# Three rewritten passages and 109 unread TensorE products in a twelve-block residual kernel on one core

## The chip, the core and the metric

The kernel runs on one core of one Trainium2 chip. The metric is the device time of one execution in microseconds (us), lower is better. The kernel before was run three times: 3741.72, 3752.7 and 3753.8 us; the median is 3752.7 us.

The engines are named as the profile names them: PE is TensorE (matrix products and transposes; PEld is its loading of weights, that is, of the operand that stays in place), DVE is VectorE, ACT is ScalarE, POOL is GpSimd, and SP is SyncE, whose queue issues most of the transfers (DMAs) between memory and the core's SBUF. Products land in PSUM, from where DVE or ACT copy ("evict") them into SBUF.

## The reference

The input `x` is [16, 64, 256], that is 1024 tokens of 256 features; there is a context `ctx_1024` of [16, 1601, 256] and a mask over it. The reference adds twelve blocks to `x`, each of a layer norm of `x`:

```python
x = x + _L0_xattn_ref(_layernorm(x), ctx, ctx, ...)    # 16 heads, softmax over the 1601 context rows
x = x + _L0_attn_ref(_layernorm(x), ...)               # 4 encoder layers, linear attention with elu + 1
x = x + _L0_ffn_ref(_layernorm(x), ...)                # 8 experts, the best 2 of each token, capacity 160
x = x + _L1_xattn_ref(_layernorm(x), ctx, ...)         # slot attention, 3 rounds with a GRU cell
x = x + _L1_attn_ref(_layernorm(x), ...)               # 16 heads, softmax over 64 tokens, own input added
x = x + _L1_ffn_ref(_layernorm(x), ...)                # 8 experts, 2 rounds of an integrator, then a refining MLP
x = x + _L2_xattn_ref(_layernorm(x), ctx, mask, ...)   # relu(score + bias)^2, normed by its sum, masked
x = x + _L2_attn_ref(_layernorm(x), ...)               # linear attention over 64 features of normed q and k
x = x + _L2_ffn_ref(_layernorm(x), ...)                # 16 experts, the best 8, and a shared one
x = x + _L3_xattn_ref(_layernorm(x), ctx, ...)         # one head of 256 over the context
x = x + _L3_attn_ref(_layernorm(x), ...)               # 16 heads, causal, with a bias by relative position
x = x + _L3_ffn_ref(_layernorm(x), ...)                # int8 quantised product
```

Three pieces matter for the change. `_L0_attn_ref` begins with `x = sqrt(256) * x_in + position_row` and a second layer norm of that (`ln1` of its first layer), so between block one and the first product of block two stand two layer norms in a row. `_L1_ffn_ref` adds to its experts' products the bias of the chosen expert (`expert_b2`, 8 x 768) or of the shared one (`shared_b2`, 768), and ends with `out = xf + integration_weight * refined`, where `refined = gelu(...) @ refine_w2 + refine_b2`. `_L3_attn_ref` adds `rel_emb[buckets]` (one number for each pair of positions and each head) to the scores and hides the keys above the diagonal.

## The kernel before, in words

The 1024 tokens are 8 tiles of 128 (`NT`), the 256 features 2 chunks of 128 (`KC`). `x` stays in SBUF for the whole program as `self.x` [128, 8, 256]. The program is one method for each block, in the order of `STAGES`; the last block (`l3_ffn`) runs inside `l3_attn`. Products and transposes are issued by `mm` (L2470) and `tr` (L2476). While `self.pinned` is true they, and the DVE, ACT and POOL instructions issued through the helper `Written` (L50 to L60), keep the order in which they are written; so a profile line of L2472, L2477 or L59 is that of a helper, and the operation is told by the names of its tiles. Each engine works through its own queue in order: an instruction that waits holds back all behind it on that engine. A tile of a pool is one of a fixed number of buffers (`bufs`) with the same tag; making the next one waits until the old one has been read.

**The two blocks that stream the context, l0_xattn (0 to 862 us) and l2_xattn (2338 to 2997 us).** Both go through `stream` (L2361). The 16 batches times 13 chunks of 128 context rows are taken in pairs, k from -9 to 103. Each round writes, in this order: `weights(k+1)` (scores of the next pair, and their exponentials or squares on ACT and DVE), in the last eight rounds one `out(t)` (the output product of token tile t, added to `x` by DVE's `add_to_x`), two `project` (keys and values of a context chunk 18 chunks ahead, evicted from the PSUM tag `bk`), `values(2k)` and `values(2k+1)` (products of the exponentials with the values, into the tag `acc`), and, in l0_xattn only, jobs `extra` (maxima for a coming batch). After the loop come the heads of the last batch and `out(7)`. Before the loop, l0_xattn norms all tiles, transposes them and makes the queries `qT`.

**l0_attn (862 to 1375 us).** The tokens are two halves, a (tiles 0 to 3) and b (tiles 4 to 7); of each half a `Half` holds `x`, `y`, `n` (the normed tiles), `hT` (the transposed ones), `kz`, `va`, `qT`, `h1T`. Steps of both halves are generators that the text lets run by turns (`go(it, n)`): `project` (L560: transposes, keys and values of each tile `kv(t)`, queries), `attend` (L605: `sums` of keys times values, `apply`, output product), `feed` (the MLP), and at the end `route` (L751: the choice of experts, in blocks g = 0 to 3 of two tiles each: a transpose `turn`, a product `gate`, ranks on DVE, a product `pos` for the places, then a scatter by POOL). The start of the block (L825 to L836) measures, scales (`start`, L704) and norms tiles 0 to 3 of a and 0, 1 of b before the first `turn`; the rest of b follows between products of `project(a)`. The weights of layer 0 and the row vectors (`rows`, `lnf`) are transferred on SP's queue as their buffers come free. A tile `zero` [128, 256] is written to all rows of `taken` (the experts' rows in memory) by one transfer.

At the end of l0_attn stands the bias by relative position for block eleven: 16 x 4 small products of one-hot rows `hot` with `rel_emb` into four PSUM banks, then 32 DVE additions of `above` (-3e38 above the diagonal) that evict them, and a transfer to memory by POOL's queue.

**l1_xattn (1400 to 1925 us)** turns the slots (`turned`), then goes through the context of all batches and ends each round with `update` (the GRU). **l1_attn (1925 to 2010 us) and l3_attn (3620 to 3740 us)** share `token_attention` (L2498): `linear(0)` norms and transposes half 0 (`tr`), makes queries and keys (`lin_t`) and values; then, for each tile t, `scores(t)`, parts of `linear(1)`, `values(t-1)` (transposes `turn` of the weights, then the products `acc`), and `project(t-2)`. In l1_attn `own_input` is true. In l3_attn a `then` object interleaves the last block: `Then.turn` (L2287, transposes `trb` of the quantised tile) and `Then.product`. **l2_attn (2997 to 3106 us)** has the same form: `linear` (L1881), `key_features`, `apply`, `sums`, `project` (L1992).

**l1_ffn (2010 to 2338 us)** loads its weights on SP's queue in the order of the code. After them it makes `bias2` [128, 768] in bf16 (L1551 to L1563): rows 0 to 23 hold the 8 experts' biases split into three bf16 parts, rows 24 to 26 the shared one. A float32 tile `raw` of 32 rows gets the biases three times, and DVE takes nine steps over 32 x 768: a copy into bf16, the rest, and a masked addition, three times. `pc`, the first product that reads it, is in `control`. `refine` (L1730) ends the block: for each tile four products `po`, DVE's addition of `fb2` (`refine_b2`), POOL's product with `iw` (`integration_weight`), DVE's addition to `x`, and the measuring of `x` for the next layer norm.

## Time and profile before

| | before |
|---|---|
| median of the runs | 3752.7 us |
| lowest and highest run | 3741.72 and 3753.8 us |
| the profiled execution | 3741.89 us |
| its span in the profile | 3740.1 us |
| mean granted clock of TensorE in it | 0.963 |
| PE busy | 3434.1 us (92%) |
| DVE busy | 1975.9 us (53%) |
| ACT busy | 1459.0 us (39%) |
| POOL busy | 1284.7 us (34%) |
| transfers | 259.71 MB, mean 69 GB/s |

A profile is that of one execution. Its slice row PEclk gives, for 40 equal stretches of the span (93.5 us each), the clock that was granted to TensorE in tenths of full speed, and the row PE its busy share; the same can be asked for any stretch. The row of a single stretch gives its bounds and length, the busy time (number of instructions) of PE, PEld, DVE, ACT, POOL and SP, then the granted clock, the busy share of the DMA engines and GB/s. A row of the timeline gives the start, the duration, the engine, the line, the operation with its tiles (output, then inputs, then partitions x elements) and the number of instructions in the group, and in brackets the idle time of the engine before it with what ended it.

### The profile page before, as it was taken

To read this page: it belongs to the slowest core of one execution; us is meant where nothing else is said; L and a number is where in the kernel's file an instruction comes from. 1 tells how busy PE (TensorE), PEld (TensorE's weight loads), DVE (VectorE), ACT (ScalarE), POOL (GpSimd) and SP (SyncE) were. 2 spreads that over 40 slices of the span, in tenths; PEclk is the share of its full clock that TensorE was granted. 3 is DMA by queue.
4 is the path that set the end of the run, shared out by engine and by line. 5 is a ranking of instruction groups with operands and counts; after the bars stand their busy time and mean duration, and the time that the engine had idled before them with its cause. 6 is when DMAs were issued, how large, how long until landed. Compare 5 with 4: busy or idle time off the path is not lost.

```text
span 3740.1 us, 70775 instructions
## 1 busy us (share of the span) xinstructions
PE 3434.1 (92%) x30951; PEld 2183.0 (58%) x30966; DVE 1975.9 (53%) x3682; ACT 1459.0 (39%) x2081; POOL 1284.7 (34%) x786
## 2 busy tenths in 40 slices
PE   8999999996999977999987998999999879999986
...
PEclk9999999998999978999998999999999979999997
...
DMA packets 106411, 259.71 MB, mean 69 GB/s; under 512 B 9235, under 2 KB 74515, under 8 KB 103798
## 3 DMA queue, kind: packets, MB, share of 16 engines
...
q14 instruction: 66, 0.54, 0.0%
...
## 4 chain that ended last, share of the span: by engine, by line
PE 49%; DVE 8%; ACT 3%; issue 2%; POOL 0%; DMA 0%; another core or an unknown queue 0%; SPq 0%; DVEq 0%; POOLq 0%; ACTq 0%
PE pk L2472 9%; PE sc L2472 8%; PE pu L2472 4%; PE acc L2472 3%; PE gate L2065 3%; PE up L2065 3%; PE lin L216 3%; PE pc L1688 3%; PE prz L2472 2%; PE gelu_t L1605 2%; PE turn L2477 2%; PE lin L2472 1%; PE pa L2472 1%; PE pn L2472 1%; DVE e L1832 1%
## 5 line engine op out<-in xcount | busy, mean ns | idle before, releaser
L2405 POOL TENSOR_TENSOR tot<-tot,e 128x1024 f32<-128x1024 f32 (+1 forms) x340 | 802.9, 2362 | 374.7 <-ACT e L349 251.5
L292 DVE TENSOR_REDUCE m<-sc 128x4 f32<-128x2048 f32 x96 | 220.1, 2293 | 272.6 <-PE sc L2472 271.5
L1832 DVE SCALAR_TENSOR_TENSOR e<-sc,row_L_xattn_nbias,free 128x2048 f32<-128x2048 f32 x104 | 244.3, 2349 | 116.5 <-PE sc L2472 114.9
L1834 ACT ACTIVATE e<-e 128x2048 f32<-128x2048 f32 x104 | 198.7, 1911 | 243.7 <-DVE e L1832 243.7
L349 ACT ACTIVATE e<-sc 128x2048 f32<-128x2048 f32 x104 | 195.2, 1877 | 242.3 <-PE sc L2472 240.7
L2472 PE MATMUL sc<-qb,kT 32*128 32x128 f32 x6656 | 245.4, 284 | 35.3 <-DVE m L306 12.4
L2472 PEld LDWEIGHTS sc<-qb,kT 32*128 32x128 f32 x6656 | 206.4, 187 | 79.7 <-issue 24.1
L2472 PE MATMUL acc<-e,v 128*32 128x128 f32 x6656 | 226.9, 276 | 7.2 <-ACT e L1835 7.2
L2472 PEld LDWEIGHTS acc<-e,v 128*32 128x32 f32 x6656 | 170.3, 110 | 106.6 <-issue 95.2
L2472 PE MATMUL pk<-cT,wk 128*128 128x512 f32 (+1 forms) x512 | 206.6, 532 | 3.6 <-DVE rows L322 3.6
L2472 PE MATMUL pk<-wv,cT 128*128 128x256 f32 x832 | 209.6, 394 | 0.0
L1835 ACT ACTIVATE e<-e 128x2048 f32<-128x2048 f32 x104 | 198.8, 1911 | 3.2
L2472 PE MATMUL pk<-wkv,cT 128*128 128x256 f32 x832 | 196.3, 386 | 0.0
L2472 PE MATMUL pk<-cT,wkv 128*128 128x512 f32 (+1 forms) x512 | 194.9, 522 | 0.0
L2472 PEld LDWEIGHTS pk<-wv,cT 128*128 128x128 f32 x832 | 149.5, 190 | 76.4 <-issue 59.0
L2472 PEld LDWEIGHTS pk<-wkv,cT 128*128 128x128 f32 x832 | 153.2, 190 | 28.5 <-issue 4.3
L2472 PE MATMUL pu<-cn,e 128*64 128x257 f32 (+1 forms) x1248 | 145.0, 389 | 12.9 <-POOL e L1240 12.9
L1688 PE MATMUL pc<-ew,eh 128*128 128x256 f32 x640 | 155.5, 385 | 0.0
L2069 ACT ACTIVATE g<-gate 128x512 f32<-128x512 f32 x68 | 40.7, 598 | 293.3 <-PE gate L2065 293.3
L2472 PE MATMUL sc<-kT,qb 32*128 32x512 f32 (+2 forms) x1536 | 141.5, 468 | 14.6 <-DVE m L292 2.3
L1230 POOL TENSOR_TENSOR e<-e,mx 128x512 f32<-128x512 f32 x96 | 81.8, 883 | 195.1 <-DVE mx L1229 195.1
L2472 PE MATMUL sc<-cT,qT 128*64 128x512 f32 (+1 forms) x768 | 142.4, 523 | 3.5 <-ACT scs L1210 3.0
...
## 6 DMA issues: line engine op xcount, KB each, us to landing
cT<-in_ctx_t SPq DMA_DIRECT2D x128, 832.0 KB
...
```

What stands on the lines that cost most here:

```text
L216: nc.tensor.matmul(pm, xT[:, k, t * P : (t + 1) * P], w[:, k, :], start=(k == 0), stop=(k == kc - 1))
L292: nc.vector.tensor_reduce(x.m4[:, g, :, i], pm, AX.X, ALU.max)
L349: nc.scalar.activation(e, pm, AF.Exp, scale=0.25)
L1230: pin(nc.gpsimd.tensor_tensor(p.e, p.e, p.mx.unsqueeze(2).to_broadcast(p.shape), ALU.subtract))
L1605: nc.tensor.matmul(pm, w[:, c, lo : lo + m], cT[:, c, :], start=(c == 0), stop=(c == nk - 1))
L1688: nc.tensor.matmul(pc[:, n, j, :], s.eh[i][:, c, tok], ew2[:, c, cols], start=False, stop=(c == 3))
L1832: nc.vector.scalar_tensor_tensor(e16, pm16, nb, free[:, at : at + P].unsqueeze(1).to_broadcast([P, 16, P]), ALU.add, ALU.mult)
L1834: nc.scalar.activation(e, e, AF.Relu)
L1835: nc.scalar.activation(e, e, AF.Square)
L2065: nc.tensor.matmul(pm[-1], w[:, k, n * P : (n + 1) * P], xT[:, k, tok], start=(k == 0), stop=(k == KC - 1))
L2405: nc.gpsimd.tensor_tensor(tot[:w], x.first if c == 1 else tot[:w], e[:w], ALU.add)
L2472: ins = self.nc.tensor.matmul(*args, **kw)
```

## The change

The change has two kinds of edits; what the program computes stays the same.

**Unread products.** A new function `awake(pool, n, tag)` takes one PSUM buffer of the pool and multiplies the identity with the first 512 columns of the constants into it, n times; nothing reads the buffer. These products are written in at 37 points of the run, each ahead of the work that PE would come to next, 109 products in all: 5 (with a tile of ones in place of the identity) ahead of the first transposes of the program, 2 before the first scores of l0_xattn, 3 (l0_xattn) and 7 (l2_xattn) in the last rounds of the stream and 3 more before each one's last `out`; in l0_attn 10 in the first layer's `project_first`, `project` and `attend` and 14 in `route`; 21 in l1_xattn; in l1_attn 4 before the transposes and 3 in `values`, in l3_attn 3 before `lin_t` and 5 in `values`; 12 in l2_attn; and 14 in `Then.turn` before tiles 0, 6 and 7.

**Three rewritten passages.**

1. The seam from l0_xattn to l0_attn. The buffers `y` and `hT` of half a and the small ones of the norms are made before l0_xattn (`begin`). `out(t)` now measures its tile; after tile 5 the roots for tiles 0 to 3 are worked out on DVE (`quick_roots`, without ACT's root) and tiles 0 and 1 are scaled and measured (`start`), after tile 6 they are normed (`norm`), after tile 7 transposed and evicted into `hT` (`turned`). In l0_attn half a begins with `project_first` in place of `project`: `kv` of tiles 0 and 1 at once, then the transposes of tiles 2 and 3, `kv` of these, then one exponential over all four tiles and the queries. The norms of tiles 2, 3 and 4 to 7 are written between its steps. The tiles are made, and the row vectors transferred, in another order; `zero` becomes [128, 128] with two transfers of half rows, and POOL's two additions of `lnf` to `x` are moved behind the first `mix`.

2. The bias by relative position. Four products of the identity with `above` start the four banks, the 64 small products add to them, and 16 ACT copies evict in place of 32 DVE additions.

3. l1_ffn. The biases are loaded first, once, in 128 rows of 54 columns, split by DVE in five steps of that size, and brought into the rows of `bias2` by two pairs of transfers through memory on POOL's queue. `fb2` is multiplied by `iw` and added to `x` by POOL in `start`, so that `refine` multiplies by `iw` as it evicts, and POOL's product is gone.

The diff, cut to its core:

```diff
+    def awake(self, pool, n, tag, bufs=None):
+        if n:
+            pm = pool.tile([P, 512], F32, tag=tag, name="awake", **({"bufs": bufs} if bufs else {}))
+            for _ in range(n):
+                self.mm(pm, self.ident, self.cst[:, :512], start=True, stop=True)

 l0_xattn
+        self.begun = self.begin(self.at_once.enter_context(tc.tile_pool(name="l0y", bufs=1, reuse_waits="tile")))
...
+            nc.vector.memset(qT[:, 0, :512], 1.0)
+            pm = ps.tile([P, 512], F32, tag="acc", name="awake")
+            for _ in range(5):
+                self.mm(pm, qT[:, 0, :P], qT[:, 0, :512], start=True, stop=True)
             self.layernorm(sb, self.x, xln)
...
             def weights(pair):
                 pm = quad()
+                if pair[0][0].b == pair[0][1] == 0:
+                    self.awake(ps, 2, "acc")
...
+            def start():
+                n = sb2.tile([P, KC, SKP], F32, tag="cT", name="n")[:, 0, : 2 * D].rearrange("p (t d) -> p t d", d=D)
+                for t in range(2):
+                    nc.scalar.activation(n[:, t], self.x[:, t, :], AF.Identity, bias=nx.less[:, t : t + 1])
+                    nc.vector.scalar_tensor_tensor(nx.y[:, t, :], n[:, t], nx.r[:, t : t + 1], pos, ALU.mult, ALU.add)
+                    nx.measure(nx.y[:, t, :], nx.mvy[:, t])
+            def norm():
+                nx.root(nx.ry, nx.mvy, 1.0)
+                for t in range(2):
+                    nc.vector.tensor_scalar(
+                        nx.n[:, t], nx.y[:, t, :], nx.mvy[:, t, 0:1], nx.ry[:, t : t + 1], ALU.subtract, ALU.mult)
+            def turned():
+                pt = ps.tile([P, KC, 2, P], F32, tag="bk", name="tr")
+                ... four transposes
+                nc.vector.tensor_scalar(to[:, 0], of[0], ln_s[:, 0:1], ln_b[:, 0:1], ALU.mult, ALU.add)
+                nc.scalar.activation(to[:, 1], of[1], AF.Identity, bias=ln_b[:, 1:2], scale=ln_s[:, 1:2])
...
             def out(t):
                 self.add_to_x(t, pm)
+                self.measured(t, False)
+                if t == 5:
+                    nx.quick_roots(0, 4)
+                    start()
+                if t == 6:
+                    norm()
+                if t == 7:
+                    turned()

 l0_attn
+            def project_first(s, w):
+                for t in range(HT):
+                    if t == 2:
+                        self.awake(ps, 1, "mm", 3)
+                        turn(s, 1, w.ln1_s, w.ln1_b)
+                        yield
+                    self.awake(ps, (1, 0, 4, 0)[t], "mm", 3)
+                    kv(t)
+                    yield
+                A.activation(s.tmp, s.kz, AF.Exp, bias=less)
+                for c in range(KC):
+                    pm = by_feature(w.wq, c, s.hT)
+                    ...
+                    yield
+                add_row(s, w.bo)
...
-            for s, n in ((a, 2), (b, 1)):
-                for p in range(n):
-                    start(s, p)
-                    measure(s, s.y, p)
-                for p in range(n):
-                    norm(s, s.y, p)
...
-            pr = project(a, w)
-            go(pr, 3)
-            measure(b, b.x, 1)
+            pr = project_first(a, w)
+            start(a, 1)
+            nx.roots(4, NT, V, A)
             go(pr, 1)
+            norm(a, a.y, 1)
+            go(pr, 1)
+            start(b, 0)
+            go(pr, 1)
+            norm(b, b.y, 0)
             start(b, 1)
...
-            at, pr = attend(a, w), project(b, w)
+            at, pr = attend(a, w, True), project(b, w, True)    # True: 2 unread products in each
...
 route
+                self.awake(ps, (3, 0, 0, 7)[g], "mm", 3)
                 turn(s, p)
...
+                self.awake(ps, (0, 3, 0, 1)[g], "mm", 3)
                 pos = ps.tile([P, 2, E], F32, tag="mm", name="pos", bufs=3, padded_shape=[P, 64, E])
 position bias
+            for r in range(4):
+                self.mm(banks[r] ..., self.ident, above[:, keys].unsqueeze(2).to_broadcast([P, 16, H]), start=True, stop=False, ...)
...
-                            V.tensor_tensor(
-                                bias[o, :, 2 * g + j, keys], of[:, g], above[o, :, keys].to_broadcast([S, 4, 16]), ALU.add)
+                        A.copy(to[:, j], of)

 l1_xattn
+            self.awake(ps, 9, "tr", 3)
             tiles[0].sT = take(turned(tiles[0].s), "sT", 2)
...
+                self.awake(ps, 0 if n else 7, "tr", 3)
                 update(sa, None, sb_ if n else None)
...
+                    self.awake(ps, 5, "tr", 3)
                 update(sb_, an and an[0])

 l1_ffn
+            raw = sb.tile([P, n8 + W // P], F32, tag="raw", name="raw")
+            ... two loads; for j in range(3): copy into part[:, j], subtract
+                nc.gpsimd.dma_start(split.rearrange("j (p c) -> p j c", p=P), part[:, :, lo : lo + n])
+                nc.gpsimd.dma_start(bias2[at : at + 3 * m], split.rearrange("j (e n) -> (j e) n", n=W))
...
 start (l1_ffn)
+                if s.i == 0:
+                    nc.gpsimd.tensor_tensor(fb2, fb2, iw, ALU.mult)
+                nc.gpsimd.tensor_tensor(s.x, s.x, fb2.unsqueeze(1).to_broadcast([P, TT, D]), ALU.add)
 refine
-                    nc.vector.tensor_tensor(y, pm, fb2, ALU.add)
-                    nc.gpsimd.tensor_tensor(y, y, iw, ALU.mult)
+                    nc.vector.tensor_tensor(y, pm, iw, ALU.mult)

 l2_attn
+                    self.awake(ps, 4 if i == 0 and t0 else 0, "mm", 2)    # before the transposes of z
+                    self.awake(ps, 2 * g, "mm", 2)                        # before pqp
+                    self.awake(ps, 0 if t else 2, "mm", 2)                # before key_features(0)
+                    self.awake(ps, 2 if t > NT else 0, "mm", 2)           # before the last project

 l3_ffn, Then.turn
+                self.awake(ps, {0: 7, 6: 4, 7: 3}.get(t, 0), "mm", 2)

 stream
+        waits = {-1: 3} if extra else {-7: 2, -5: 1, -4: 1, -1: 3}
                 if h and k >= 0:
+                    self.awake(ps, waits.get(k - N // 2, 0), "bk")
                     values(2 * k)
...
         finish(xs[B - 1])
+        self.awake(ps, 3, "bk")
         out(NT - 1)

 token_attention
+            if i == 0:
+                self.awake(ps, 4 if own_input else 0, "mm", 2)            # before the transposes
+                if n == i == 0:
+                    self.awake(ps, 0 if own_input else 3, "mm", 2)        # before lin_t
+            self.awake(ps, ({1: 2, 2: 1} if own_input else {2: 1}).get(t, 0), "mm", 2)     # values, before turn
+            self.awake(ps, 0 if own_input else {1: 1, 2: 1, 5: 2}.get(t, 0), "mm", 2)      # values, before acc
```

## The prediction

> **What bounds the kernel now.** I read the page's busy table and slices first, then the chain that ended last, then the stretches of 1 and 2 us around each dip of the clock, then the timeline of TensorE (PE) there.
>
> ```profile
> span 3740.1 us, 70775 instructions
> PE 3434.1 (92%) x30951; PEld 2183.0 (58%) x30966; DVE 1975.9 (53%) x3682; ACT 1459.0 (39%) x2081; POOL 1284.7 (34%) x786
> ...
> PE   8999999996999977999987998999999879999986
> ...
> PEclk9999999998999978999998999999999979999997
> ...
> PE 49%; DVE 8%; ACT 3%; issue 2%; POOL 0%; DMA 0%; another core or an unknown queue 0%; SPq 0%; DVEq 0%; POOLq 0%; ACTq 0%
> ```
>
> PE is busy 92% and leads the chain; two things eat the rest: about 306 us in which PE is idle, and the low slices of the clock row, at the seams between stages. In 1 us stretches, PE's busy time times the missing share of the clock sums to 99 us over 34 dips: an upper bound for what a clock that never falls could give. One dip in full:
>
> ```profile
> 60.00:62.00 2.00, 2.00 (x11) 0.61 (x10) 0.86 (x5) 0.33 (x1) 0.00 (x0) 1.00 0.05 20
> 62.00:64.00 2.00, 0.75 (x3) 0.10 (x1) 1.77 (x4) 1.25 (x2) 0.00 (x0) 1.00 0.00 0
> 64.00:66.00 2.00, 0.44 (x13) 0.47 (x17) 1.41 (x1) 0.61 (x1) 0.00 (x0) 1.00 0.00 0
> 66.00:68.00 2.00, 2.00 (x36) 1.68 (x28) 0.00 (x0) 0.00 (x0) 0.00 (x0) 0.54 0.03 8
> 68.00:70.00 2.00, 2.00 (x8) 0.80 (x7) 0.00 (x0) 1.25 (x1) 0.00 (x0) 0.61 0.00 0
> 70.00:72.00 2.00, 2.00 (x11) 0.50 (x9) 0.00 (x0) 1.21 (x2) 1.30 (x1) 1.00 0.00 0
> ```
>
> First number after the stretch's length is PE, third from last the clock. PE waits from 62.75 to 65.56, and then works at about half clock for 3.4 us: 1.7 us lost after the wait is over. These waits recur:
>
> ```profile
> 65.56 1.60 PE L2472 MATMUL sc<-qb,kT 32*128 32x128 f32 x32 [2.81 <-DVE m L292]
> ...
> 870.12 0.48 PE L2477 MATMUL tr<-cst,n 128*128 128x128 f32 x1 [5.71 <-DVE n L59]
> ...
> 880.21 6.24 PE L2472 MATMUL lin<-wkv,hT 128*128 128x512 f32 x8 [7.35 <-DVE hT L59]
> ...
> 2039.50 0.40 PE L1681 MATMUL pc<-bias,shared 128*128 128x256 bf16 x1 [7.27 <-DVE bias L1563]
> ...
> 3629.01 3.70 PE L2472 MATMUL lin_t<-xT,wqkv 128*128 128x512 f32 x8 [0.80 <-ACT qb L2549]
> ...
> 3725.25 0.88 PE L2477 MATMUL trb<-identb,f_xq 128*128 128x128 bf16 x4 [4.18 <-ACT f_xq L2283]
> ...
> 3730.07 0.39 PE L2477 MATMUL trb<-identb,f_xq 128*128 128x128 bf16 x2 [0.26 <-ACT f_xq L2283]
> ```
>
> **The price of one unread product.** A float32 product with 512 columns is two records. In the row at 3629 their weights follow each other every 0.43 us at full clock, in the row at 880 every 0.85 at half: 0.86 or 1.71 us a product. I count 109 of them. 78 stand where this trace has a wait of PE, of 86 us together: 67 us at full clock, 78% of the waits. In a wait they cost nothing, since the releaser (a DVE, ACT or POOL chain) doesn't depend on PE; where there is no wait they cost 0.86 each.
>
> **Joined part 1, the seam from l0_xattn to l0_attn.** Before: last product of the stream ends 864.40, first key product 880.21, layer 0's first `sums` 911.06. That head start is the layer norms (DVE and ACT, 863 to 880) of six token tiles, done in a block. After: tiles 0 and 1 are normed during the last three `out` calls, so the first key product waits for four transposes (0.6) and two evictions (0.54 and 0.56) after the last `add_to_x`: about 866.5, 14 us sooner. From there to `sums` PE has 8 key, 2 query and 16 transposing products, 16 us warm; the waits for the norms of tiles 2, 3 and of the second half, interleaved, I put at 8 us, against 13 before. So `sums` comes near 891 to 893: 19. Against it: five more DVE and ACT steps stand in the tail of the stream (ACT's last `exp` ends 857.29, the values need it at 857.9: no slack), and three products stand before those values, 2.6 at most. Value 17, ends 8 (the row of b vectors again lands at 868.7, as now, and four products run after it) and 25. The zeros written in two half rows on SP's queue at 12.8 are read only after 1303; POOL's two additions of 2.5 us moved behind `mix` are read at the last layer.
>
> **Joined part 2, the position bias.** 32 DVE additions (4.55 us) become 16 ACT copies (nearest row: 128x256 copied in 0.37; 16 of half that size about 4) and four identity products (256 columns, 2 records of 0.23 each: 1.8). PE's 128 little products before them take 9.4 at half clock. With seven unread products in the 7.18 us wait before 1345.73, the gate, position and bias products run warm: 1.2 + 2.0 on the chain to the scatter, some 4 before the eviction. The next wait (1367 to 1374, for DVE's copy of xsT) has behind it a softmax that stood until 1369.7 for something the trace does not name; if it is the transfer of the bias, it comes sooner too. Value 4, ends -2 and 8.
>
> **Joined part 3, l1_ffn.** The 7.27 us wait at 2039.50 is DVE's splitting of a 32x768 bias (nine steps of 0.55 to 1.0). In a 128-partition layout the steps are 54 columns wide (nearest rows: 0.15 to 0.2), and two trips through memory follow on POOL's queue; even issued as late as 2006.6, where the raw bias is loaded now, four hops of some 2.5 us end before 2032. Then routing's chain (softmax, ranks: about 5 us on DVE) is next, partly beside four `pc` products: 7, ends 3 and 9. In `refine` the POOL product (0.64 plus two hand-overs) leaves a serial chain of 2.2 us per tile; 1.45 remains, under PE's 1.77: the last tile ends 2 sooner, ends 1 and 2.5. POOL's new addition of 2.35 twice lies before `vn`, which is not read until 2045.
>
> **Unread products in real waits.** Loss of the dip each prevents, discounted a little: stream's start at 66 1.7; routes 1291 5 (of 6.3) and 1318 1.5; l1_xattn 1438 1.5 and 1911 2.2; l1_attn 1929 2.8 and 1966 1.5; end of l2_xattn 2991 2.5; l2_attn 3015 2, 3025 2.6, 3069 3.8, 3107 1; l3_attn 3671 3, 3690 1.5, 3703 2.5. Sum 35. At the start of the program and at 1412.78 (nine products in 8.75) I take 0.5 each: after 1412 ACT stands until 1423.4 on an unnamed queue with the DMA engines full. 36, ends 15 and 50.
>
> **Unread products where I find no wait.** End of l2_xattn: two and one where PE waits 0.57 and 0: 1.5. Between the two transposes and `acc` of value tile 5 of l3_attn: the filler needs the PSUM buffer that ACT empties only at 3703.0, so two start when `acc` could: 1.5. `attend` of layer 0: two, 1.7. The program's end: four before the transposes of tile 6 (row at 3730.07: 0.26 of wait; the 4.18 is before tile 4) and three before tile 7, which must then wait for tile 6's product: about 4. Sum 9, ends 2 and 16.
>
> **Sum.** 17 + 4 + 7 + 2 + 36 - 9 = 57. From this 3 for waits not filled (2.98 at 2101, 2.39 at 2306) that may now fall into a bad phase of the clock: 54. The profiled execution took 3741.89 (span 3740.1 and 1.8 around it): 3688. It is at the lower end of the runs shown (3741.72 to 3753.8, median 3752.7); a median of runs spread like that can lie up to 11 higher, which the upper end takes in.
>
> By the Trainium skill, "TensorE: Matmul & The Clock Gate", section "HAM oscillation — how this bites in real kernels", only idle gaps over about 3.4 us are to be avoided. Then the fillings of 2 to 3 us would give nothing, some 17 less: 3705. The row at 65.56 speaks against it: 2.81 us of wait, and the clock at 0.54 behind it.
>
> **Rivals.** (a) PE stays warm, but the chains of DVE and ACT end the stages anyway (l2_attn, l3_attn: ACT `e`, DVE `rec` 1.76 in each step), so half of the 36 goes back into waits: gain 54 - 18 = 36, and with a seam at its low end 27, about 3712. For: 88 us of waits behind ACT and DVE remain on the chain. Against: after most of these dips PE runs without a wait. (b) Everything fills: 25 + 8 + 11 + 45 - 5 = 84, 3658. (c) Slower: identity products do not hold the clock. Then the 78 take 133 us at half clock in 86 us of waits, 47 over, and the other 31 up to 53 instead of 9; minus the 30 of the joined parts, about 3770 with some of it hidden. It decides from 1.1 us per product on, where 78 fill 86. Against it: PE enters each wait at full clock, which falls only 1 to 4 us later, and transposes by the same identity run amid clock 1.00 (1453 to 1900). (d) No change: seam at 8, filled waits at 15, losses at 16, about 12.
>
> **Chances.** Forecast (gain 40 to 72) 0.58; (a) 0.23; (b) 0.09; (c) 0.07; (d) 0.03. Faster by over 0.3% (11 us, about what can be told) 0.90, same 0.03, slower 0.07. The range leaves out the far half of (b), (c), (d) and little of (a): 3658 to 3728.
>
> **What would show it.** Mean clock from 0.963 to about 0.98. No dip after 66, 1291, 1929, 3015, 3069; dips left at 1374, 2014, 2247, 2339, 3472. First key product within 4 us of the stream's last product; no wait for DVE `bias` in l1_ffn. The rows of the unread products: 0.43 a record. Wrong if they read 0.85, if waits before the same instructions are as long behind the fillers, or if the seam waits on a row transfer.

## The result, and the profile after

The changed kernel's median is 3730.05 us over eight runs (3726.93 to 3733.56); the kernel before, on the same chips, has 3742.65 (3740.18 to 3754.37). The ratio is 0.9969, with a 95% interval from 0.9957 to 0.9981: 12 us faster, where 54 were forecast. The time lies 2 us above the upper end of the range. The profiled execution took 3730.16 us; its span is 11.7 us shorter than that of the kernel before. Executions of one kernel can lie in two groups some 10 to 13 us apart (of ten of `joined_only`, told below, three took 3727 to 3731, one 3735 and six 3741 to 3743), so that a median also says which group was met more often, and I read stretches from the profiled executions.

Of the page of the kernel after, the busy row, the slice row of the clock and the shares of the chain that ended last:

```profile
span 3728.4 us, 71203 instructions
...
PE 3499.4 (94%) x31177; PEld 2200.2 (59%) x31192; DVE 1970.9 (53%) x3645; ACT 1461.2 (39%) x2093; POOL 1286.4 (35%) x784
...
PEclk9999999999999979999999999999999989999998
...
PE 75%; DVE 13%; ACT 7%; issue 2%; DMA 1%; POOL 0%; SPq 0%; ACTq 0%; DVEq 0%; POOLq 0%
```

The clock did what was forecast: its mean is 0.979, and of the low slices three are left, at 7 around 1305 to 1398 us and at 8 around 2983 to 3076 and at the end. PE's busy time went *up* by 65 us, although the only products added that anything reads are the four of the position bias. The dip that the prediction showed in full, in the same view, is gone:

```profile
62.00:64.00 2.00, 1.57 (x4) 0.38 (x2) 2.00 (x2) 1.65 (x2) 0.00 (x0) 1.00 0.00 0
64.00:66.00 2.00, 1.40 (x37) 1.31 (x38) 0.45 (x1) 0.00 (x0) 0.00 (x0) 1.00 0.04 8
66.00:68.00 2.00, 2.00 (x15) 0.95 (x12) 0.00 (x0) 1.28 (x1) 0.00 (x0) 1.00 0.00 0
```

To see where the time went I summed three things over the span in stretches of 1 us: PE's busy time, its idle time, and busy time times the missing share of the clock (the loss by the clock). `joined_only` is the kernel after without its unread products; `squares_first` and `joined_squares` are the same pair with one more edit.

| | span | PE busy | PE idle | loss by the clock |
|---|---|---|---|---|
| before | 3740.1 | 3434.0 | 306.1 | 98.8 |
| joined_only | 3729.3 | 3438.2 | 291.1 | 99.1 |
| after | 3728.4 | 3499.4 | 229.0 | 60.6 |
| joined_squares | 3716.9 | 3436.2 | 280.7 | 96.8 |
| squares_first | 3716.9 | 3501.5 | 215.4 | 61.0 |

From `joined_only` to the kernel after the loss by the clock falls by 38.5. Busy time nevertheless rises by 61.2, so the unread products themselves take 61.2 + 38.5 = 99.7 us, counted at full clock. Idle time falls by 62.1 only. The remaining 37.6 us of unread products did not lie in idle time: they were added to the path, and they eat the 38.5 that the clock gave. The other pair says the same: 35.8 gained by the clock, 101.1 of products, 65.3 less idle time, a span that is equal to 0.1 us.

By stretch of the program (us from the first product of one block to that of the next, PE's timeline; the profiled executions). The last two rows part at l3_attn's first `lin_t`, so its first transposes, and the three unread products ahead of that `lin_t`, count to the row above:

| stretch | before | joined_only | after | joined_squares | squares_first | pruned | all_three |
|---|---|---|---|---|---|---|---|
| start to layer 0's first `sums` | 911.1 | 901.6 | 895.9 | 901.7 | 897.7 | 897.4 | 894.5 |
| to the first `gate` | 384.0 | 385.3 | 386.0 | 384.4 | 386.0 | 383.0 | 383.0 |
| to the first `hidden` of l0_ffn | 79.0 | 89.3 | 82.8 | 74.9 | 69.3 | 82.9 | 68.2 |
| to the first `prz` of l1_xattn | 71.9 | 66.8 | 66.1 | 68.7 | 65.5 | 65.5 | 69.2 |
| to l1_attn | 483.8 | 483.8 | 481.8 | 484.2 | 481.7 | 481.7 | 481.9 |
| l1_attn | 81.9 | 80.9 | 86.6 | 81.4 | 86.1 | 82.6 | 84.4 |
| l1_ffn | 326.6 | 321.7 | 320.8 | 321.7 | 321.9 | 321.1 | 321.7 |
| l2_xattn | 659.8 | 658.7 | 659.9 | 658.7 | 660.1 | 659.9 | 657.6 |
| l2_attn | 109.2 | 109.1 | 114.7 | 109.1 | 114.7 | 112.6 | 109.9 |
| l2_ffn and l3_xattn | 517.2 | 517.2 | 518.1 | 517.2 | 518.1 | 517.5 | 517.4 |
| l3_attn to the end | 115.6 | 114.8 | 115.7 | 114.9 | 115.7 | 112.1 | 112.0 |

Stretches of equal text differ between executions by up to about 3 us (l2_xattn 657.6 or 660; more in l2_attn and l3_attn, told at the end), so a single row is weak evidence below that, and differences that recur in several pairs are what I go by.

Three rows carry the story. The seam gave 15 us, and 9.5 of it without any unread product. The way to `hidden` became 10 us *longer* by the joined changes. And l1_attn and l2_attn became 5 to 6 us longer by the unread products, though 13.7 us of loss were to be prevented there.

### The profile page after: what moved, and what is told of

Read it like the earlier page. It is cut to its first block, busy times and chain, and to the rows that moved or that the text cites. A ratio compares the mean times of both kernels' runs of the same rounds, so it can differ in the third digit from the quotient of the medians.

```text
span 3728.4 us, 71203 instructions
## 1 busy us (share of the span) xinstructions
PE 3499.4 (94%) x31177; PEld 2200.2 (59%) x31192; DVE 1970.9 (53%) x3645; ACT 1461.2 (39%) x2093; POOL 1286.4 (35%) x784
## 4 chain that ended last, share of the span: by engine, by line
PE 75%; DVE 13%; ACT 7%; issue 2%; DMA 1%; POOL 0%; SPq 0%; ACTq 0%; DVEq 0%; POOLq 0%
PE sc L2619 15%; PE pk L2619 15%; PE lin L2619 6%; PE acc L2619 6%; PE lin_t L2619 5%; ACT e L358 5%; PE pu L2619 4%; PE gate L2166 3%; PE up L2166 3%; PE lin L216 3%; PE pc L1786 3%; PE prz L2619 2%; PE gelu_t L1700 2%; PE turn L2631 1%; PE pa L2619 1%
## 5 line engine op out<-in xcount | busy, mean ns | idle before, releaser
L1786 PE MATMUL pc<-ew,eh 128*128 128x256 f32 x640 | 156.1, 386 | 0.0
L1319 POOL TENSOR_TENSOR e<-e,mx 128x512 f32<-128x512 f32 x96 | 81.9, 885 | 194.3 <-DVE mx L1318 194.3
L2171 DVE TENSOR_TENSOR hT<-up,g 128x512 f32<-128x512 f32 x68 | 47.0, 691 | 183.2 <-PE up L2166 183.2
## 6 DMA issues: line engine op xcount, KB each, us to landing
piece<-in_ctx_n ACTq DMA_DIRECT2D x16, 384.0 KB, 3.7
```

The source lines that it names most:

```text
L1319: pin(nc.gpsimd.tensor_tensor(p.e, p.e, p.mx.unsqueeze(2).to_broadcast(p.shape), ALU.subtract))
L1786: nc.tensor.matmul(pc[:, n, j, :], s.eh[i][:, c, tok], ew2[:, c, cols], start=False, stop=(c == 3))
```

## The experiments

All kernels compute the whole reference. Where nothing else is said, the edit is to the kernel after, and "gain" is against the kernel before.

| kernel | median, us | ratio to before [95%] | profiled span | clock |
|---|---|---|---|---|
| after | 3730.05 | 0.9969 [0.9957, 0.9981] | 3728.4 | 0.979 |
| joined_only | 3741.54 | 0.9988 [0.9975, 1.0002] | 3729.3 | 0.964 |
| joined_again | one execution: 3732.26 | | 3730.5 | 0.963 |
| fillers_only | 3736.21 | 0.9986 [0.9976, 0.9997] | 3731.9 | 0.978 |
| squares_first | 3718.74 | 0.9934 [0.9914, 0.9954] | 3716.9 | 0.980 |
| joined_squares | 3719.12 | 0.9957 [0.9941, 0.9973] | 3716.9 | 0.965 |
| bias_on_dve | one execution: 3729.08 | | 3727.3 | 0.978 |
| pruned | 3717.98 | 0.9933 [0.9910, 0.9957] | 3716.2 | 0.975 |
| root_on_dve | 3729.10 | 0.9965 [0.9952, 0.9978] | 3727.7 | 0.978 |
| all_three | 3703.79 | 0.9895 [0.9867, 0.9924] | 3699.7 | 0.977 |
| all_three_again | 3703.21 | 0.9907 [0.9894, 0.9920] | 3698.0 | 0.977 |
| other_buffer | 3704.73 | 0.9905 [0.9890, 0.9921] | 3701.2 | 0.979 |
| best | 3710.57 | 0.9916 [0.9902, 0.9931] | 3696.0 | 0.978 |
| best_again | one execution: 3710.11 | | 3708.3 | 0.973 |
| best_with_l1 | 3704.46 | 0.9893 [0.9875, 0.9911] | 3695.0 | 0.979 |
| best_with_l2 | 3695.81 | 0.9866 [0.9845, 0.9887] | 3699.1 | 0.977 |

### The two halves of the change, one at a time

`joined_only`: the three rewritten passages without the unread products.

```diff
     def awake(self, pool, n, tag, bufs=None):
-        if n:
+        if False:
...
-            nc.vector.memset(qT[:, 0, :512], 1.0)
-            pm = ps.tile([P, 512], F32, tag="acc", name="awake")
-            for _ in range(5):
-                self.mm(pm, qT[:, 0, :P], qT[:, 0, :512], start=True, stop=True)
```

> The kernel after without any unread product; the three joined passages stay. Theory A (the unread products win about as much by the clock as they take on the path, so the whole gain of 12 us is the joined passages'): 0.9967 of the time before, 3730, with TensorE busy at low clock for about 85 us (99 before, 61 after). Theory B (the joined passages gain nothing by themselves, since their waits only move, and the unread products made the gain): within 4 of the time before, 3740 to 3746. Theory C (the joined passages would gain what was forecast, 30, and the unread products lose 18 of it): about 3713. In every theory l1_ffn tells of joined part 3 by itself, and the stretch from the last product of the stream to layer 0's first sums of joined part 1.

`fillers_only`: the kernel before with 103 of the unread products, at the same places.

```diff
+    def awake(self, pool, n, tag, bufs=None):
+        if n:
+            pm = pool.tile([P, 512], F32, tag=tag, name="awake", **({"bufs": bufs} if bufs else {}))
+            for _ in range(n):
+                self.mm(pm, self.ident, self.cst[:, :512], start=True, stop=True)
...
+                self.awake(ps, (3, 0, 0, 7)[g], "mm", 3)
                 turn(s, p)
...
+        waits = {-1: 3} if extra else {-7: 2, -5: 1, -4: 1, -1: 3}
```

> The kernel before with the unread products alone, at the same points (without the six in project_first, which it does not have: 103). Theory A: within 4 of the time before, 3739 to 3747, with TensorE's idle time down by about 60 us and its busy time up by as much; busy at low clock down to about 60 to 70 us. Theory B: 12 faster, about 3731. Theory C: 18 slower, about 3760. If waits lengthened behind the unread products by as much as the clock saves (the chains of the other engines set the ends), idle time plus the unread products' 89 us would be above the idle time before (306) by about 30.

Measured: `joined_only` 10.8 us shorter in the profiled execution, its median not to be told from before; `fillers_only` 8.2 shorter in the profile, ratio 0.9986. Each half was to bring about 30 and 27. So two things had to be found: why the rewritten passages give a third of what was forecast, and why the unread products give a third although the clock rises as forecast.

By its profile `joined_only` stands where theory A put it (3730), by its median where theory B did (3741.54). All eight executions of the kernel after lie at 3727 to 3734; of `joined_only` six of ten lie at 3741 to 3743, and the means are 3730.7 and 3737.5. The same holds for the pair with the squares first, told below: five executions of `squares_first` at 3713 to 3720, three of seven of `joined_squares` at 3729 to 3733, means 3717.7 and 3723.3. So against a short execution, and that is what the profiles compare, the unread products bring nothing; over the executions they bring some 6 us, since the long ones did not occur with them. `fillers_only` agrees: 3734 to 3740, where six of the 19 executions of the kernel before on that chip lie at 3745 to 3753. No long execution of `joined_only` or `joined_squares` was profiled, so where its 12 us lie is not known. (Not all these kernels ran on one chip; the kernel before has medians of 3739.0 to 3742.7 on them.) In `fillers_only` the sums are as theory A had them: idle time falls from 306.1 to 236.8, busy time rises from 3434.0 to 3495.2, and the loss by the clock falls from 98.8 to 60.4.

### Why l0_ffn starts late: SP's loads behind ACT's squares

The row of the table from `gate` to `hidden` is 10.3 us longer in `joined_only`. SP's own waits in the kernel after, from 1310 to 1368 us (total, number of times, longest), and its timeline there:

```profile
SPq L1057 <- ACT junk L59: 38.2, 1, 38.2
```

```profile
1350.31 4.12 SPq L1057 DMA_DIRECT2D w<-in_L_ffn_W  x8
...
1356.89 0.38 SPq L1066 DMA_DIRECT2D xs<-taken  x1
```

The loads of the experts' weights stand for 38 us until ACT has done its last `junk` (the squares of context rows that l1_xattn needs later, written there as the last work of l0_attn, `squares(999)`). Behind the loads, in the same queue, stands the transfer `xs` of the tokens that POOL has scattered, and for that PE waits. Before, the weights were issued at 1330.88 without that wait. ACT's timeline of the kernel after shows what is late:

```profile
1343.49 3.47 ACT L59 COPY kept<-pb 64x128 f32<-64x128 f32 x16 [15.44 <-PE pb L2619]
1346.99 0.42 ACT L59 ACTIVATE junk<-piece 128x256 bf16<-128x256 f32 x1
...
1349.79 0.40 ACT L59 ACTIVATE junk<-piece 128x256 bf16<-128x256 f32 x1
```

The 16 new copies of the position bias wait 15.44 us for PE at the head of ACT's queue, and the eight last squares stand behind them, with nothing to wait for themselves.

`squares_first`: the squares are written ahead of the bias.

```diff
             go(route(b, 1))
+            squares(999)
             banks = ps_kv.tile([P, 2, 512], F32, tag="kv", name="pb")
...
             nc.gpsimd.dma_start(self.position_bias, bias.rearrange("p r g s -> p (r g s)"))
-            squares(999)
             self.pinned = False
```

> The kernel after with one line moved: in l0_attn the last squares of the context (ten on ACT) are written before the products of the position bias and not after their 16 ACT copies. Theory D (SP's loads of layer 0's expert weights wait for the last square, which now stands behind the copies, and the gathers of the tokens queue behind these loads, so joined part 2 costs what joined part 1 gains): the loads start near 1332 in place of 1350, the first hidden product comes 9 to 13 sooner, near 1353, and the time falls by 8 to 12, ratio to the kernel before 0.994. Rival E (the gathers wait for the scatter or for the weights' transfer anyway, the wait before them only changes its name): within 3 of the kernel after. Against it stands that the scatter is issued by 1339.

PE's timeline, first of the kernel after, then of `squares_first`, whose SP queue issues the weights at 1333.12 and `xs` at 1346.09:

```profile
1362.26 1.08 PE L2631 MATMUL tr<-cst,xs 128*128 128x128 f32 x4 [18.81 <-DMA xs<-taken]
...
1364.72 2.50 PE L2619 MATMUL hidden<-xsT,w 128*128 128x160 f32 x8 [0.52 <-DVE xsT L127]
```

```profile
1350.35 1.09 PE L2631 MATMUL tr<-cst,xs 128*128 128x128 f32 x4 [8.40 <-DMA xs<-taken]
...
1353.02 2.50 PE L2619 MATMUL hidden<-xsT,w 128*128 128x160 f32 x8 [0.51 <-DVE xsT L127]
```

`hidden` begins 11.7 us sooner, and the whole span is 11.5 shorter; the ratio goes from 0.9969 to 0.9934, with intervals that do not meet. One moved line is worth as much as the whole change had brought.

`bias_on_dve` undoes joined part 2 alone.

```diff
-            for r in range(4):
-                keys = slice(16 * r, 16 * r + 16)
-                self.mm(
-                    banks[r][:, : 16 * H].rearrange("p (k h) -> p k h", h=H), self.ident,
-                    above[:, keys].unsqueeze(2).to_broadcast([P, 16, H]), start=True, stop=False, skip_group_check=True)
...
-                    for j in range(2):
-                        A.copy(to[:, j], of)
+                    for g in range(KC):
+                        for j in range(2):
+                            V.tensor_tensor(
+                                bias[o, :, 2 * g + j, keys], of[:, g], above[o, :, keys].to_broadcast([S, 4, 16]), ALU.add)
```

> The kernel after with joined part 2 undone: the position bias is evicted by 32 DVE additions again and ACT does its last squares at once. Theory D: SP's loads still wait for the last square (they did not before the change, so it is the new layout of the buffers that lets them wait), but that square ends near 1331: the loads start there, the first hidden product comes between 1350 and 1358 in place of 1364.7, so joined part 2 costs 7 to 14 by its place in ACT's queue. Rival (the loads wait for the layout alone): hidden near 1365 again.

SP's loads still wait for `junk`, but 19.1 us and until 1336.85, since ACT now reaches the squares at once; `hidden` begins at 1355.73, and the stretch takes 68.3. The total is only 1.1 shorter than after: `sums` came 4.0 later there (tail of the stream, ahead of the edit), the way to `gate` 1.5 and to `prz` 4.5 longer. So what costs the time is the order on ACT. That the loads wait for `junk` at all is new with the joined changes; the new pool `l0y` and the other order of tiles would explain it, but I made no kernel with the old layout and the rest, so this part is argued.

`joined_squares` is `joined_only` with the squares first (the same line moved), and `joined_again` is one more execution of `joined_only` on the same chip.

> The joined passages without any unread product, with the last squares of the context written ahead of the position bias. Theory D: 9 to 13 faster than joined_only (profile 3729.3): 3717 to 3721, so that the joined passages by themselves are worth some 20 and the unread products next to nothing in the kernel after. Rival: the gain of squares_first needs the unread products' earlier routing; then within 4 of joined_only.

> The kernel of joined_only once more, one look: its ten times lay at 3727 to 3731 (three), 3735 and 3741 to 3743 (six), and the profile shown was of one of the short ones. If this execution is one of the long ones, the 12 us more should stand at one place (theory: one long wait or a dip of the clock that holds on), or be spread over many dips (rival: the clock falls at more places).

Spans 3716.9 and 3730.5, medians as in the table (`joined_again` was not one of the long executions): with the squares first the joined changes alone bring 23 us in the profile, and the 109 unread products on top of it nothing in this pair of profiles (3716.9 again). Stretch by stretch they gain 13.7 up to l1_attn (4.0 at the seam, 5.6 at `hidden`, 3.2 at `prz`, 2.5 in l1_xattn, less 1.6 before `gate`) and lose the same after it (4.7 in l1_attn, 5.6 in l2_attn, 1.4 in l2_xattn, and some 2 elsewhere).

### Why the unread products bring so little: the buffer they write

In l1_attn, the place before the transposes `turn` of the weights. PE's timeline in `joined_only`, and its 2 us stretches (PE's busy time first, clock third from last):

```profile
1959.26 1.99 PE L2615 MATMUL lin<-wqkv,xT 128*128 128x256 f32 x8
1963.34 1.30 PE L2627 MATMUL turn<-cst,e 128*128 128x128 f32 x8 [2.09 <-DVE vm L2716]
```

```profile
1961.00:1963.00 2.00, 0.26 (x2) 0.00 (x0) 2.00 (x4) 0.00 (x0) 0.00 (x0) 1.00 0.00 0
1963.00:1965.00 2.00, 1.65 (x37) 1.28 (x40) 0.59 (x3) 1.89 (x3) 0.00 (x0) 0.76 0.00 0
1965.00:1967.00 2.00, 2.00 (x123) 1.60 (x105) 0.03 (x1) 0.26 (x1) 0.00 (x0) 0.50 0.04 8
```

This is a real wait of 2.09 us with a fall of the clock behind it, and two unread products (four records) were to fill it. The same place in the kernel after:

```profile
1947.48 1.99 PE L2619 MATMUL lin<-wqkv,xT 128*128 128x256 f32 x8
1951.55 2.40 PE L2619 MATMUL awake<-cst 128*128 128x512 f32 x4 [2.08 <-DVE vm L2720]
1953.75 1.92 PE L2631 MATMUL turn<-cst,e 128*128 128x128 f32 x8
```

```profile
1952.00:1954.00 2.00, 2.00 (x6) 0.84 (x5) 0.00 (x0) 0.30 (x1) 0.00 (x0) 0.73 0.00 0
1954.00:1956.00 2.00, 2.00 (x40) 1.67 (x38) 0.00 (x0) 0.89 (x2) 0.00 (x0) 0.50 0.04 8
```

The wait is as long as it was, the clock falls as it did, and the unread products stand *behind* the wait, where they add 2.2 us. The reason is in the call: `self.awake(ps, ..., "mm", 2)` takes one of the two PSUM buffers of the tag `mm`, and `turn` is waiting for just such a buffer, until DVE has evicted `vm` from it. The unread product asks for it first, and waits for it in `turn`'s stead.

`pruned` takes out 25 of the 109 products, 14 at places where the timeline showed them starting only when the wait ended, and 11 where the wait was judged too short or absent.

```diff
-                    self.awake(ps, (1, 0, 4, 0)[t], "mm", 3)
+                    self.awake(ps, (0, 0, 4, 0)[t], "mm", 3)
...
-                self.awake(ps, 2 if early else 0, "mm", 3)
                 turn(s, 0)
...
                 if t > 1:
-                    self.awake(ps, 2 if t > NT else 0, "mm", 2)
                     project(t - 2)
...
-                self.awake(ps, {0: 7, 6: 4, 7: 3}.get(t, 0), "mm", 2)
+                self.awake(ps, {0: 7}.get(t, 0), "mm", 2)
...
-        waits = {-1: 3} if extra else {-7: 2, -5: 1, -4: 1, -1: 3}
+        waits = {-1: 3} if extra else {-5: 1, -4: 1, -1: 3}
...
             for n in range(4):
-                if n == i == 0:
-                    self.awake(ps, 0 if own_input else 3, "mm", 2)
...
-            self.awake(ps, ({1: 2, 2: 1} if own_input else {2: 1}).get(t, 0), "mm", 2)
             for g in range(KC):
...
-            self.awake(ps, 0 if own_input else {1: 1, 2: 1, 5: 2}.get(t, 0), "mm", 2)
             acc = ps.tile([P, 2, 512], F32, tag="acc", name="acc", bufs=1)
```

> The kernel after without 25 of its 109 unread products: those that waited for a PSUM buffer themselves (values and lin_t of l1_attn and l3_attn, the last project of l2_attn, one in project_first) or stood where TensorE did not wait (attend, round -7 of l2_xattn, the last two tiles of Then.turn). Theory F (a product that needs the buffer that the wait is for starts when the wait is over and lies whole on the path): 25 times 0.86 is 21 us less work on the path, less some 8 dips of 1.6 that come back: 5 to 13 faster than after, ratio to before 0.992 to 0.995. Rival G (what they hold of the clock is worth what they take): within 3 of the kernel after. Rival H (they are worth more than they take): 5 or more slower than after.

12.2 us shorter than after, median 12.1 less, and the gain stands where products were taken out: 3.0 before `gate`, 4.0 in l1_attn, 2.0 in l2_attn, 3.7 in l3_attn. In the sums PE's busy time falls by 15.7 while the loss by the clock rises by 6.8 (to 67.4), so 22.5 us of products are gone. Idle time rises by 3.5 only (to 232.5): 19.0 of the 22.5 had lain on the path, and the clock takes 6.8 of that back.

At the end of the program four of the products stand before tile 6, where PE waits only 0.26 us, and three before tile 7. PE's timeline of `joined_only`, then of the kernel after, from the transposes of the quantised tile 6 on:

```profile
3719.24 0.39 PE L2627 MATMUL trb<-identb,f_xq 128*128 128x128 bf16 x2 [0.26 <-ACT f_xq L2380]
3720.15 0.61 PE L2615 MATMUL f_lin<-wb,f_qT 128*128 128x256 bf16 x2 [0.52 <-DVE f_mv L2360]
3724.05 0.40 PE L2627 MATMUL trb<-identb,f_xq 128*128 128x128 bf16 x2 [3.30 <-ACT f_xq L2380]
```

```profile
3715.28 4.77 PE L2619 MATMUL awake<-cst 128*128 128x512 f32 x8
3719.88 0.28 PE L2631 MATMUL trb<-identb,f_xq 128*128 128x128 bf16 x2
...
3720.85 2.74 PE L2619 MATMUL awake<-cst 128*128 128x512 f32 x6
3723.42 0.28 PE L2631 MATMUL trb<-identb,f_xq 128*128 128x128 bf16 x2
```

From the first `trb` of tiles 4 and 5 (3714.42 and 3710.93) to that of tile 7 it takes 9.63 us without and 12.49 with the seven products. To tile 6 it takes 4.82 and 8.95, so the four before tile 6 cost 4.1; the three before tile 7 stand where `joined_only` waits 3.30, and 1.3 comes back there.

In l2_attn, 5.6 us longer than in `joined_only`, the buffer is the smaller part (2.1 by `pruned`, two products ahead of the last `project`). Up to the `pk` shown here the stretch is 0.5 us longer (82.5 from its first product, for 82.0), although the clock loses 6.9 less in it; the other 5.0 arise behind. PE's, POOL's and DVE's timelines of the kernel after:

```profile
3062.40 3.62 PE L2619 MATMUL pk<-va,kp 64*128 64x33 f32 x32 [5.15 <-DVE kp L2055]
...
3051.49 10.81 POOL L2041 TENSOR_SCALAR qp<-qp 128x2048 f32<-128x2048 f32 x2 [17.55 <-ACT qp L2040]
...
3060.51 1.82 DVE L2055 TENSOR_SCALAR kp<-pkp 128x1024 f32<-128x1024 f32 x1
```

PE waits 5.15 us for `kp`, and DVE's `kp` ends at 3062.33, when POOL's two additions to `qp` end (3062.30). In `joined_only` both end together too, at 3070.0; PE, colder up to there, then waits only 0.78. Why `kp` ends with POOL's additions the traces do not say. So at this place the time that the clock gave became a wait behind POOL, and behind that wait the clock is at 0.50 until 3069. The 5.15 stand in every profile with l2_attn's ten products ahead of it (`after`, `fillers_only`, `squares_first`, `bias_on_dve`, `pruned`, `root_on_dve`, `all_three` and its repeat, `other_buffer`, `best_with_l2`), and at most 1.03 in those without.

### A root on ACT in the tail of the stream

The seam's other cost. `norm()`, which the joined changes put after `out(6)`, takes ACT's square root. ACT's timeline of the kernel after:

```profile
848.82 1.88 ACT L358 ACTIVATE e<-sc 128x2048 f32<-128x2048 f32 x1 [1.56 <-POOL tot L2548]
850.72 1.28 ACT L2475 ACT_TABLE_LOAD   x1
857.04 0.20 ACT L2475 ACTIVATE ry<-ry 128x2 f32<-128x2 f32 x1 [5.04 <-DVE ry L2474]
857.26 1.28 ACT L358 ACT_TABLE_LOAD   x1
858.56 1.88 ACT L358 ACTIVATE e<-sc 128x2048 f32<-128x2048 f32 x1
```

The stream's last exponential `e` stands in ACT's queue behind a root of 0.20 us that waits 5.04 for DVE, and behind a second load of the function table. Before, that `e` ran from 855.41; here from 858.56, and in `joined_only` from 860.98. By the Trainium skill, "ScalarE: Activation LUTs", section "What ACT_TABLE_LOAD costs", a switch to another table takes about 2.66 us in all, 1.28 the load and 1.38 a drain; here the next activation starts 0.02 us after the load of 1.28, so the trace shows 1.30.

`root_on_dve` works the root out on DVE, as `quick_roots` does, and leaves away the three unread products that stood in the wait it caused.

```diff
             def norm():
-                nx.root(nx.ry, nx.mvy, 1.0)
+                nx.quick(nx.ry, nx.mvy[:, :, 1], 1.0)
...
+        def quick(r, var, scale):
+            V = nc.vector
+            vq = pool.tile([P, 2, 4], F32, tag="vq", name="vq")
+            v, q = vq[:, 0, : r.shape[1]], vq[:, 1, : r.shape[1]]
+            V.tensor_scalar(v, var, 1e-5, scale, ALU.add, ALU.mult)
...
-        waits = {-1: 3} if extra else {-7: 2, -5: 1, -4: 1, -1: 3}
+        waits = {} if extra else {-7: 2, -5: 1, -4: 1, -1: 3}
```

> The kernel after with the root of the second norm in the stream's tail (ry) worked out on DVE, as the first already is, in place of ACT's square root, and without the three unread products in l0_xattn's round -1. Theory I (ACT's root stands in front of the last exponential and brings two loads of its table, so the last values come 5 us late, which the unread products only cover): the last values start near 858 to 859 in place of 860.5, the first key product 2 to 3 sooner; 2 to 4 faster than after. Rival (DVE, which has ten more steps, becomes the bound of the tail): within 1 or slower.

The last `e` now starts at 854.81, 3.75 sooner, and the values that need it no longer wait. But the first transposes of the next block start only 0.9 sooner (865.90 for 866.76), since DVE's chain is next, and `sums` 2.1 sooner. In the total 0.7 us: l1_attn takes 90.8 in this execution, 4 more than in the kernel after with the same text. Most of that stands behind one stall: PE is idle for 1.50 us in the midst of a group of `acc`, until 1975.32, for nothing that the profile names; the clock falls to 0.50 behind it, and the four records of the next `lin` take 2.08. The like stall of the kernel after is 0.81, and its `lin` takes 1.13. Such stalls are taken up at the end.

### The three repairs together, and the unread products put into another buffer

`all_three`: `squares_first`, `pruned` and `root_on_dve` in one kernel, 81 unread products (their diffs stand above). `all_three_again` is the same kernel on another chip.

> The three edits together. If theories D, F and I hold and the places do not touch each other: 15 to 28 faster than after, 3702 to 3715, ratio to before 0.990 or below. If only D holds: 8 to 12 faster.

> The three edits together once more, beside other_buffer on the same chip: 0.987 to 0.992 of the kernel before.

28.7 us shorter than after in the profile and 26.3 by the medians, where the three measured singly add up to 24.4 in the profiles; the repeat agrees (3703.21).

`other_buffer` puts back 11 of the products that `pruned` had taken out of l1_attn and l3_attn, but into the PSUM buffer of the tag `acc`, which the transposes do not wait for.

```diff
+    def awake_in(self, pool, n):
+        if n:
+            pm = pool.tile([P, 2, 512], F32, tag="acc", name="awake", bufs=1)
+            for _ in range(n):
+                self.mm(pm[:, 0, :], self.ident, self.cst[:, :512], start=True, stop=True)
...
+            self.awake_in(ps, ({1: 2, 2: 1} if own_input else {2: 1}).get(t, 0))
             for g in range(KC):
...
+            self.awake_in(ps, 0 if own_input else {1: 1, 2: 1, 5: 2}.get(t, 0))
             acc = ps.tile([P, 2, 512], F32, tag="acc", name="acc", bufs=1)
```

> The three edits together, and 11 of the taken-out unread products of l1_attn and l3_attn put back at their places, but into the PSUM buffer of acc, which the wait there is not for. Theory F (only the buffer made them cost): they start when TensorE's work ends and lie inside the wait, for instance two between 1933.7 and 1935.8 in l1_attn, after which turn starts as late as without them; those before acc, whose wait is for ACT's copy, likewise; the time is that of the three edits less some dips of 1.6: 0 to 6 faster than all_three. Rival G2 (it is their length, not the buffer): they lie on the path here too, 11 times 0.86, some 6 to 9 slower than all_three.

PE's timeline of `other_buffer` at the place in l1_attn shown above, and its stretches:

```profile
1929.25 1.99 PE L2621 MATMUL lin<-wqkv,xT 128*128 128x256 f32 x8
1931.08 1.88 PE L2621 MATMUL awake<-cst 128*128 128x512 f32 x4
1933.32 1.06 PE L2640 MATMUL turn<-cst,e 128*128 128x128 f32 x8 [0.37 <-DVE vm L2729]
```

```profile
1931.00:1933.00 2.00, 1.96 (x6) 0.62 (x4) 2.00 (x4) 0.00 (x0) 0.00 (x0) 1.00 0.00 0
1933.00:1935.00 2.00, 1.44 (x40) 1.16 (x40) 0.57 (x3) 1.99 (x3) 0.00 (x0) 1.00 0.00 0
1935.00:1937.00 2.00, 1.97 (x112) 1.69 (x100) 0.68 (x1) 0.06 (x1) 0.00 (x0) 1.00 0.03 8
```

This is what the change was meant to look like: the products start at once, 0.37 of the wait is left, and the clock stays at 1.00. `turn` takes 1.06 in place of 1.30 and 1.92, but that alone proves little: in `all_three`, with no product there and a wait of 2.08, it takes 1.06 too, and the clock falls just behind it (0.85, 0.50 and 0.79 in the three 2 us stretches from 1936, some 1.7 us of loss). That dip is what the two products save. At this place the mechanism is shown; its worth is small. Against `all_three` l1_attn is 1.0 and l3_attn 4.0 shorter, but l2_xattn and l2_attn, whose text is the same in both, are 2.9 and 2.7 longer, and the medians are equal (3704.73 and 3703.79): the 6 to 9 us slower of rival G2 are ruled out, but of the forecast gain nothing stands in the medians.

### Which products in the later blocks are worth keeping

`best` (a name given ahead of the run): `other_buffer` without those of l1_attn (4 before the transposes, 3 in `values`), the 3 before `lin_t` in l3_attn and 10 in l2_attn; 72 products. `best_with_l2` puts l2_attn's ten back, `best_with_l1` the four before l1_attn's transposes, and `best_again` is one more execution of `best`. The last three ran on another chip than `best`.

```diff
-                    self.awake(ps, 4 if i == 0 and t0 else 0, "mm", 2)
...
                 for g in range(KC):
-                    self.awake(ps, 2 * g, "mm", 2)
...
-                    self.awake(ps, 0 if t else 2, "mm", 2)
                     kp = key_features(t)
...
-            if i == 0:
-                self.awake(ps, 4 if own_input else 0, "mm", 2)
...
-                if n == i == 0:
-                    self.awake_in(ps, 0 if own_input else 3)
...
-            self.awake_in(ps, ({1: 2, 2: 1} if own_input else {2: 1}).get(t, 0))
+            self.awake_in(ps, 0 if own_input else {2: 1}.get(t, 0))
```

> The three edits, with 72 unread products: none in l1_attn and l2_attn, and in l3_attn the five of values in the buffer of acc, the three before lin_t left out. If a stretch's unread products are worth what the stretch shows with and without them (l1_attn 80.9 to 81.4 without any, 84.4 in all_three; l2_attn 109.1 without, 109.9; l3_attn 108.0 with the products in the buffer of acc, 112.0 in all_three): 6 to 9 faster than all_three, profile near 3691, ratio to before 0.988. Rival (these stretches differ between kernels by where the clock's fall lies in them, not by the unread products): within 3 of all_three, 3700 to 3706.

> best once more, one look: if this execution is one of the long ones (3710 to 3714), the 12 us should stand in one stretch against the profile of 3696.0: l2_attn under theory J, l1_attn under K.

> best with the four unread products of l1_attn before its first transposes put back. Theory K: all times within 3696 to 3707, median near 3701. Theory J: two groups as with best, median 3708 to 3714. If both runs lie in two groups, it takes both or something else makes the groups.

> best with the ten unread products of l2_attn put back (four before the transposes of z, two before each second pqp, two before the first key_features). Six executions of best lay at 3698 and 3701 (two) and 3710 to 3714 (four), those of all_three and other_buffer at 3696 to 3707. Theory J (the products of l2_attn keep a fall of the clock from lying there in part of the executions, which costs 12): all times within 3694 to 3706, median near 3700, 8 to 10 shorter than best's 3710.6. Rival K (it is the four of l1_attn): times in two groups as with best, median 3708 to 3714.

`best` has a short profile, 3696.0, but a worse median than `all_three`: two of its six executions took 3698 and 3701, four 3710 to 3714. `best_with_l1` ran 3696.65 to 3708.19, `best_with_l2` 3690.10 to 3700.96, with the lowest median of all: 3695.81, ratio 0.9866, 34 us below that of the kernel after. Its profiled execution is one of the longer two of its four (3700.8 and 3701.0; the others 3690.8 and 3690.1). It is the fastest version found.

Neither J nor K fits: both kernels have times apart by 10 us (3690 and 3701; 3697 and 3704 to 3708), so it takes both, or something else. Whether l2_attn's ten products make `best_with_l2` the fastest I can't say. In the profiles that stretch takes 109.1, 109.1 and 110.4 us without them in `joined_only`, `joined_squares` and `best` (115.4 in the long execution `best_again`), and 112.6, 109.9, 112.7 and 112.7 with them in `pruned`, `all_three`, `other_buffer` and `best_with_l2`: they do not shorten the place where they stand, where 9.4 us of loss were to be prevented. What the medians show is that four executions with them lie at 3690 to 3701, and four of six of `best` at 3710 to 3714 (`best_again` too); but `best_with_l1`, which lacks them as well, has none above 3708.2. These are few executions, and the cause is open.

In l1_attn the four products before the transposes have a clear price. From the first transpose to the first `lin_t` it takes 2.64 us before and in `joined_only`, 2.60 in `best`, but 4.47 after, 4.46 in `all_three` and 4.47 in `best_with_l1`. DVE's timeline shows why: directly ahead of the copy of `xT` that `lin_t` needs, in `joined_only` a group of three `xln` takes 1.05 (from 1927.15), in the kernel after one of four takes 3.41 (from 1912.90). The order of DVE's instructions there is not written out by hand, and it came out differently with the added products.

## Why the prediction was wrong

**The price of an unread product: right.** Eight records take 3.70 us (2997.59 in the kernel after) and four 1.98 (3004.40): 0.43 for each further record, and the 109 together 99.7 for the 94 that 109 times 0.86 make; where the other 6 come from I did not trace.

**The clock: right in sum.** Forecast 0.98 and 36 us of loss prevented; measured 0.979 and 38.5. By place it was mixed. The dip at 66 is gone, and so are that of 1291 to 1306 in `route` and those of 3015 and 3025 in l2_attn; the one before l1_attn still stands, now at 1915 to 1923, and l2_attn is at 0.5 from 3031 to 3049 and from 3062 to 3069, the latter behind the wait for `kp`. Rival (c), that identity products do not hold the clock, is refuted as a general statement, but a filled wait is no guarantee: in the kernel after 6.17 us of unread products run until about 1325.8, two waits of 0.79 and 0.68 follow, and in the 1 us stretch from 1328 the clock is 0.64, then 0.50 until 1369, with PE idle from 1343 to 1362. Whether the phase of the gaps or the unread products' own weight for the clock decides there was not tried.

**"In a wait they cost nothing", and so only 9 us of unread products on the path: the step that failed.** Measured 37.6 (35.8 in the other pair), 28.6 more. The end of the program, one of the four places that the prediction did price, can be read by itself: put at 4, it cost 2.9. What failed is the other list. I took each product that stands where the trace of before has a wait of PE as lying in that wait, since "the releaser (a DVE, ACT or POOL chain) doesn't depend on PE". That is true and not enough: the releaser frees the very buffer that the unread product wants. For one tile, value tile 5 of l3_attn, the prediction said so (the filler needs the buffer that ACT empties) and did not ask it of the other places. The question for each call was which tag it takes, not how long the wait is.

How much of the 28.6 this is: `pruned` took 19.0 us from the path with 25 products. 13 of them are among the 14 that the prediction priced at 8.7 in all; the other 12 all waited for a buffer, and at 0.86 each they are 10 us. Of the 18.6 that `pruned` left, some 8 stand in l2_attn (9.3 by the same sum over that stretch, less 1.4 that `pruned` took), where the wait for `kp` behind POOL takes back what the clock gave, and 1.8 is the order on DVE before `lin_t`. The rest, some 9, is not assigned to places. The prediction's own count had a hole besides: of 31 products outside the waits it priced 14 in the 9, and three at the seam; the other 14, 12 us at 0.86, it left at nothing without a reason.

**Joined part 2, +4 with ends -2 and 8: wrong in sign.** From the first `gate` to the first `prz` the joined changes cost 5.2 (150.9 to 156.1). The forecast costed the ACT copies at their own 4 us (measured 3.47) and named the chain to the scatter, but not what is queued behind them on ACT: eight squares for which SP's weight loads wait, and `xs` behind these. With the squares first the same part gains 7.4 (143.5), inside the ends. So the mechanism was right, and the queue was missed. Nor did the gate, position and bias products run warm, for which 1.2 + 2.0 on the chain and some 4 before the eviction were put down: behind the seven unread products they run at 0.50 (the second half's last `gate` takes 1.73, 1.88 before).

**Joined part 1, +17: 15.1 at `sums`,** inside its ends, but a third of it came with the unread products (9.5 without). The first key product follows the last `out` by 3.7 us, as forecast (within 4). PE's timeline of the kernel after:

```profile
860.49 0.65 PE L2619 MATMUL acc<-e,cst 128*32 128x128 f32 x16 [0.38 <-ACT e L358]
...
865.83 1.10 PE L2619 MATMUL lin<-wo,xT 128*128 128x256 f32 x4 [0.17 <-DVE xT L2433]
866.76 0.60 PE L2631 MATMUL tr<-cst,n 128*128 128x128 f32 x4
868.60 1.13 PE L2619 MATMUL awake<-cst 128*128 128x512 f32 x2 [1.23 <-ACT hT L390]
869.56 3.60 PE L2619 MATMUL lin<-wkv,hT 128*128 128x512 f32 x8
...
895.94 0.73 PE L2619 MATMUL pk<-va,kz 64*128 64x136 f32 x8
```

The forecast allowed 2.6 at most for the three unread products in the stream's tail and no number for the steps added there, though it saw no slack; the last `e` is 3.2 late (5.6 in `joined_only`), since a root costs two table loads and a wait for DVE in ACT's queue. In the row at 868.60 two records wait for the buffer of `hT`'s eviction: the same fault once more.

**Joined part 3, 7 + 2: 4.9 in `joined_only`.** The wait for `bias` is gone: the product is 16.3 sooner (2039.50 to 2023.17), 12.4 of it within the block. What is late next is DVE's `hots`, as the prediction said, but with 3.7 us of waiting and not "partly beside four `pc` products", which are over by then (the kernel after):

```profile
2021.90 0.27 PE L1779 MATMUL pc<-bias,shared 128*128 128x256 bf16 x1
...
2026.28 0.62 PE L1731 MATMUL hotT<-identb,hots 128*128 128x128 bf16 x8 [3.67 <-DVE hots L1726]
```

**The rule of the skill on the clock.** By the Trainium skill, "TensorE: Matmul & The Clock Gate", section "HAM oscillation — how this bites in real kernels", only idle gaps over about 3.4 us cost the clock. The prediction set this aside, and the rows of `joined_only` above bear that out: 2.09 us of wait, then 0.76 and 0.50. So waits of 2 to 3 us were worth filling; where the buffer was the wrong one, they were not filled.

**The rivals.** (d), no change by a low sum, comes to the right number (12) with the wrong parts, which besides add up to 17 with the other terms as they stand: seam at 8, filled waits at 15, losses at 16, where the seam gave 15, the clock 38 and the losses were 38, with 5 lost on the way to l1_xattn. (a), the clock's gain handed back as waits for DVE and ACT, did not happen in the sum: idle time fell by 62. In l2_attn, which it named, idle time fell too (from 20.6 in `joined_only` to 18.2, the loss by the clock from 17.9 to 14.1, while busy time rose by 8.0), but there the wait of 5.15 for `kp` is what (a) describes, with POOL as the engine behind it. No rival named the buffer.
